# Two attention blocks on one core: which parts of x go by transfer in two jobs, and when other work is placed

## The chip, the core and the metric

The kernel runs on one core of a Trainium2 chip. The core has five engines, which run their own instruction streams and wait for each other on semaphores: TensorE (PE in the profile, with PEld for its weight loads), VectorE (DVE), ScalarE (ACT), GpSimd (POOL) and SyncE (SP, which here only issues transfers). The metric is the device time of one execution in microseconds (us), and the median of several runs is quoted.

## What is computed

The input x has 8 images of 512 channels and 32 x 32 = 1024 positions, in fp32. Two layers run one after the other, and both have the same form:

```
xn  = group_norm(x, 8 groups) * gamma + beta
q, k, v = Wq xn + bq, Wk xn + bk, Wv xn + bv      (512 x 512 weights)
a   = softmax(q^T k / 8) for each of 8 heads of 64 channels, over 1024 positions
x   = x + Wp (a v) + bp
```

All values are fp32. The result is x after the second layer.

## The kernel before

**Jobs.** A job is one image in one layer, and there are 16. Images are taken in pairs, so the order is image 0 layer 0, image 1 layer 0, image 0 layer 1, image 1 layer 1, then images 2 and 3, and so on. Jobs are numbered from 0; jobs 0 and 1 are layer 0 and jobs 2 and 3 are layer 1 of the first pair. The image stays in SBUF (the tile x) between its two layers.

**The loop.** Round n of the main loop runs the attention of job n and then the projections around it: v of job n+1 (`v_phase`), and in `deep_phases` the output projection of job n together with k and q of job n+1. Round -1 has only the projections of job 0.

**Projections by fewer products.** Each 512 x 512 projection is done in the manner of Strassen and Winograd: seven products of half size in place of eight, from sums of blocks of the input and of the weight. `FACTOR` numbers the seven weight factors. The k, q and output projections do this twice: the outer level has seven chains, taken in the order `OUTER = (1, 2, 6, 5, 7, 3, 4)`, and each chain has seven products of 128 x 256 matmuls in the order `ORDER = (1, 5, 6, 2, 7, 3, 4)`. `prepare` makes the inner factors of a weight on DVE (four sums, lines L152 to L158) at its first use, and stores them in DRAM, from where `fetch` loads them later.

**Chains, turns and queues.** A chain c fills a tile p of two halves (`put`: ACT copies two of the four quarters out of PSUM, DVE adds the other two, lines L607 and L609). In `deep_phases` two chains are always interleaved, so that a new chain begins every seven products. In its product numbers 7 and 3, which are the fifth and sixth in `ORDER`, a chain gives one turn each to other work:

```python
if ORDER[j] in (7, 3):
    if soon:
        soon.popleft()()
    elif outer:
        outer.popleft()()
    elif extra and extra[0][0] <= c:
        extra.popleft()[1]()
```

The queue `soon` holds block sums that later chains need: four steps of the inner sums (L394 to L400) and four of the output's block sums (L491 to L496). The queue `outer` holds the adds that put the outer level's results together. The queue `extra` holds loads, the output bias (`make_out_bias`, line L1023) and the norm's statistics of the job after next (line L229), each with the first chain in which it may run. What is left of `extra` runs early in the next attention.

**Outer results of the output projection.** When chain o ends, its part is added to the residual x. x has four quarters (channel half, position half). Part 1 and part 2 go to (0,0); parts 6 + 1, 5 and 3 to (0,1); parts 7 + 6 + 1 and 4 to (1,0); parts 7 + 6 + 1 and 5 to (1,1). `more(oh, sh, part, moved)` adds a part to a quarter, in one of two ways: with `moved` it issues at once a transfer on GpSimd's queue that accumulates into SBUF (line L636); without it, it queues a DVE add (line L638) in `outer`. The sums "p6 += p1" and "p7 += p6" are DVE adds in `outer` too (line L622). In layer 1 a quarter that has all its parts is sent to the output.

**Order.** PE, ACT and DVE execute in the order in which the Python code emits (`manual_schedule`), and the framework puts in the waits that the data need, in that order of emission. So an instruction that is emitted after another one on the same data waits for it, though it be a transfer. A call `later(t, fn)` emits fn once a clock, advanced by hand with each product, has moved on by t.

**Attention.** 64 steps, i = 0 to 63: PE makes the scores of step i (L817), ACT the exponential into a tile e (L822, one of six buffers), DVE adds e into acc (L832, L834), and PE multiplies by v two steps later (L848). Every eight steps end a group (L864, L871), and every two groups share a normalisation (L891 to L925). Other work comes between as chores, which `put(i, fn)` places at step i or the next free one. In round 0 these are: factors of two weights (L152 to L158), the norm of job 1 (by ACT's sums L239 and L247, then `groups`, L270 to L280, `factors`, and four `apply`, L295), the four block sums of the normed input (`sums`, L356 to L362), and the second half of the inner sums (L394 to L400).

Of the kernel before, what the change touches and what calls it, by code (L numbers as in the profile page):

```python
# [70 lines left out]
def fast_path(  # L71
# [34 lines left out]
    def later(delay, fn):  # L106
        todo.append((clock[0] + delay, fn))
# [93 lines left out]
    def used(key):  # L201
        del held[key]
        later(2.5, fetch)
# [4 lines left out]
    def x_tile(b):  # L208
        xs[b] = xpool.tile([P, NC, S], F32, tag="x", name=f"x_{b}")
        return xs[b]  # L210

    def load_x(b):
        for cc in range(NC):
            nc.sync.dma_start(xs[b][:, cc, :], x[b, cc * P : (cc + 1) * P, :])

    class Norm:
# [20 lines left out]
        def sums(self, cc):  # L237

            nc.scalar.activation(  # L239
                xn[0][:, cc, :], xs[self.b][:, cc, :], AF.Identity, accum_out=self.mv[:, cc, 0:1]  # L240
            )
# [289 lines left out]
    def deep_phases(n, extra, outs=None, early=()):  # L531
# [8 lines left out]
        def job(which):  # L540
            return n - 1 if which == O else n
# [71 lines left out]
        def end(c):  # L613
            which, o = chains[c]
            m = job(which)
            used((m, which, o))

            def p(k):
                return tiles[which, k]

            def add(to_, a, b):
                outer.append(lambda: nc.vector.tensor_add(to_, a, b))  # L622

            if which == O:
                b, layer = jobs[m]
                xt = xs[b]

                def more(oh, sh, part, moved=False):


                    cols = slice(sh * HALF, (sh + 1) * HALF)
                    to_ = xt[:, 2 * oh : 2 * oh + 2, cols]

                    def go():
                        if moved:
                            nc.gpsimd.dma_start(to_, p(part), accum_op=ALU.add)  # L636
                        else:
                            nc.vector.tensor_add(to_, to_, p(part))  # L638
                        parts[oh, sh] -= 1
                        if layer == 1 and parts[oh, sh] == 0:  # L640
                            rows = slice(oh * CH, (oh + 1) * CH)
                            later(8.0 if moved else 2.0, lambda: nc.sync.dma_start(
                                out[b, rows, cols].rearrange("(c p) s -> p c s", p=P), to_
                            ))

                    if moved:
                        go()
                    else:
                        outer.append(go)

                if o == 1:
                    more(0, 0, 1, True)
                elif o == 2:
                    more(0, 0, 2, True)
                elif o == 6:
                    add(p(6), p(6), p(1))
                    more(0, 1, 6)
                elif o == 5:
                    more(0, 1, 5)
                    more(1, 1, 5, m in (0, 2))  # L660
                elif o == 7:
                    add(p(7), p(7), p(6))
                    more(1, 0, 7)
                    more(1, 1, 7)
                elif o == 3:
                    more(0, 1, 3, True)
                elif o == 4:
                    more(1, 0, 4, True)
                return
            d = dst[which]  # L670

            def quarter(oh, sh):
                return d[:, 2 * oh : 2 * oh + 2, sh * HALF : (sh + 1) * HALF]

            if o == 2:
                add(quarter(0, 0), p(1), p(2))
            elif o == 6:
                add(p(6), p(6), p(1))
            elif o == 5:
                add(quarter(0, 1), p(6), p(5))  # L680
            elif o == 7:
                add(p(7), p(7), p(6))
                add(quarter(1, 1), p(7), p(5))
            elif o == 3:
                add(quarter(0, 1), quarter(0, 1), p(3))
            elif o == 4:
                add(quarter(1, 0), p(7), p(4))

        live, parts = {}, {(0, 0): 2, (0, 1): 3, (1, 1): 2, (1, 0): 2}
        soon, outer = deque(early), deque()  # L690
# [24 lines left out]
        at = sorted((7 * c + 2 * j, c, j) for c in range(len(chains)) for j in range(7))  # L715
        return [thunk(c, j) for _, c, j in at]

    def last_weights(n):
        w = acts.tile([P, NW, 2, CH], F32, tag="deep", name="w_last")
        nc.sync.dma_start(w, factors[O, jobs[n][1]])  # L720
        return w
# [10 lines left out]
    def last_sums(sh):  # L732


        def start():
            if sh == 0:
                tx[0] = acts.tile([P, 3, 2, HALF], F32, tag="t", name="t_last")
            nc.vector.tensor_sub(last_right(sh, 5), last_right(sh, 7), last_right(sh, 1))

        def second():  # L740
            nc.vector.tensor_sub(last_right(sh, 6), last_right(sh, 3), last_right(sh, 5))

        def third():
            nc.vector.tensor_sub(last_right(sh, 7), last_right(sh, 3), last_right(sh, 7))

        def fourth():
            nc.vector.tensor_sub(last_right(sh, 4), last_right(sh, 2), last_right(sh, 6))

        return start, second, third, fourth
# [424 lines left out]
    for n in range(-1, len(jobs)):  # L1174
        last = n + 1 == len(jobs)
        outs = None
        if n >= 0:
            chores = {}

            def put(i, fn):  # L1180
                while i in chores:
                    i += 1
                chores[i] = fn

            if last:
                w = last_weights(n)
                for i, fn in enumerate(last_sums(0)):
                    put(44 + 3 * i, fn)
            else:
                if n == 0:  # L1190
                    first_factors(put, [(O, 0), (V, 1)])
                elif n == 1:
                    first_factors(put, [(K, 1), (Q, 1)])
                elif n == 2:
                    first_factors(put, [(O, 1)])
                for i, (_, fn) in enumerate(extra):
                    put(2 + i, fn)
                at = (10, 19, 22, 24, 26, 28, 36, 39, 42, 45)
                if n == 0:
                    for i, fn in zip((3, 3, 4, 5, 6, 8, 10, 11, 12, 13, 15), reads):  # L1200
                        put(i, fn)
                    at = (22, 30, 34, 35, 37, 38, 41, 44, 47, 50)
                for i, fn in zip(at, steps + sums(n + 1)):
                    put(i, fn)
                deep_first = deep_steps(n + 1)
                for at, fn in zip((52, 54, 57, 59), deep_first[4:]):
                    put(at, fn)
                put(61, lambda: (extend_plan(n + 1), [fetch() for _ in range(RING)]))
            assert max(chores, default=0) < NT * len(att.groups)
            att.run(chores)  # L1210
            banks(0, "one")
            banks(1, "one")
            if last:
                for i, fn in enumerate(last_sums(1)):
                    later(4.1 + 1.5 * i, fn)
                later(9.9, judge)
                for sh in range(2):
                    last_proj(n, w, sh)
                break
            outs = OutputSums(n)  # L1220
            out_sums(n, outs)
            first = v_phase(n + 1, ORDER)
            for thunk in first[:-1]:
                thunk()
            rest = first[-1:]
            extra = deque()
            if jobs[n][1] == 1 and jobs[n][0] + 2 < B:
                extra.append((11, lambda b=jobs[n][0] + 2: (x_tile(b), load_x(b))))
            if n == 1:
                load, bias_steps = make_out_bias(1)  # L1230
                extra.append((8, load))
                extra.extend((11, fn) for fn in bias_steps)
            if n + 2 < len(jobs):
                reads, steps = norm_steps(n + 2)
                extra.extend((15, fn) for fn in reads)
        both = deep_phases(n + 1, extra, outs, deep_first[:4] if outs else ())
        both[0]()
        rest[0]()
        if n < 0:
            later(22.0, lambda: load_x(1))  # L1240
        for thunk in both[1:-2]:
            thunk()
        banks(0, "two")
        att = Attention(n + 1)
        att.scores(0)
        att.scores(1)
        for thunk in both[-2:]:
            thunk()
        banks(1, "two")
# [249 lines left out]
```

## Time and profile before

| | |
|---|---|
| median of 3 runs | 3214.52 us (3211.47 to 3215.15) |
| profiled execution | 3210.9 us, TensorE clock 0.999 |
| PE busy | 3191.5 us (99%), 22918 matmuls |
| DVE busy | 2774.8 us (86%), 3978 instructions |
| ACT busy | 1904.5 us (59%) |
| POOL busy | 99.4 us (3%), of which 62 transfers of 512 KB into x take 74.6 to issue |
| DMA | 313.82 MB, mean 98 GB/s |

The busy time of PE counts matmuls that overlap, so it is not a measure of how near PE is to its peak. It is still the engine that hardly stops: its waits for other engines add up to 13.6 us, and none of them lies between 692 and 3170 us. DVE is the next engine, and its busy share is an average over stages in which it is full and stages in which it is not. A row of the timeline gives start, length, engine, line, operation, output<-inputs and shapes; square brackets behind it tell how long the engine had been idle, and what released it.

### The profile page before, as it was taken

The numbers are of one execution on the slowest core, as the hardware profiler recorded it, in microseconds if no ns is written. First come the engines' busy times: TensorE is split into PE (matmuls) and PEld (weight loads), VectorE is DVE, ScalarE is ACT, GpSimd is POOL, SyncE is SP. The second block draws the span as 40 slices with busy tenths as digits, with TensorE's granted clock in tenths as the row PEclk, the third lists the DMA queues.
The fourth block names the chain that finished last, engine by engine and source line by source line (L and its number), as shares of the span: only waits on it lengthen the run. The fifth ranks groups of instructions, "written<-read, shape, count | busy, mean of one in ns | idle before, by whom it ended". The sixth has DMA issues, their size and how long they took to land.

```text
span 3210.9 us, 57782 instructions
## 1 busy us (share of the span) xinstructions
PE 3191.5 (99%) x22918; PEld 1859.8 (58%) x22918; DVE 2774.8 (86%) x3978; ACT 1904.5 (59%) x3042; POOL 99.4 (3%) x93
## 2 busy tenths in 40 slices
PE   9999999999999999999999999999999999999999
PEld 7366384563836638366483754837547375573744
DVE  8897998979889798897978889788897888978878
ACT  4746646466565665656656565565656656566564
POOL 0000000000000000000000000000000000000000
PEclk9999999999999999999999999999999999999999
DMA  9234172350613305033160421504216051150511
GB/s 316 97 104 129 68 211 70 92 170 22 210 28 88 91 27 159 22 103 128 33 208 18 115 70 34 151 16 137 100 44 194 16 138 47 49 136 19 171 37 42
DMA packets 150230, 313.82 MB, mean 98 GB/s; under 512 B 33992, under 2 KB 48960, under 8 KB 148800
## 3 DMA queue, kind: packets, MB, share of 16 engines
q1 hardware_dynamic: 133088, 277.55, 26.7%
q0 software_dynamic: 16864, 32.51, 6.2%
q8 instruction: 181, 2.97, 0.4%
q14 instruction: 97, 0.79, 0.1%
HBM read 225.13 MB, written 51.18 MB: 86 GB/s over the span
## 4 chain that ended last, share of the span: by engine, by line
PE 93%; DVE 5%; DMA 1%; issue 0%; ACT 0%; SPq 0%; POOL 0%; DVEq 0%
PE sc L817 27%; PE po L848 27%; PE vd L593 10%; PE zd L593 10%; PE z L462 6%; PE ud L593 4%; PE yd L593 4%; PE v L462 2%; PE y L462 2%; PE u L462 2%; DVE acc L834 1%; DMA x<-p 0%; PE z_last L761 0%; DVE w L154 0%; DVE p L609 0%
## 5 line engine op out<-in xcount | busy, mean ns | idle before, releaser
L822 ACT ACTIVATE e<-sc 128x1024 f32<-128x1024 f32 x1024 | 1045.7, 1023 | 582.5 <-PE sc L817 488.2
L817 PE MATMUL sc<-q,k 64*64 64x512 f32 x8192 | 1061.9, 590 | 0.0
L848 PE MATMUL po<-e,v 64*64 64x512 f32 x8192 | 1057.3, 589 | 0.0
L834 DVE TENSOR_TENSOR acc<-acc,e 128x1024 f32<-128x1024 f32 x768 | 936.1, 1219 | 57.5 <-ACT e L822 8.8
L848 PEld LDWEIGHTS po<-e,v 64*64 64x64 f32 x8192 | 313.2, 133 | 565.7 <-issue 558.4
L817 PEld LDWEIGHTS sc<-q,k 64*64 64x64 f32 x8192 | 309.9, 133 | 558.9 <-issue 545.2
L593 PE MATMUL vd<-deep,w 128*128 128x256 f32 x900 | 252.7, 380 | 1.4 <-DVE p L609 1.3
L593 PE MATMUL zd<-deep,w 128*128 128x256 f32 x892 | 248.4, 380 | 4.4 <-DVE p L607 2.4
L832 DVE TENSOR_TENSOR acc<-e,e 128x1024 f32<-128x1024 f32 x128 | 156.3, 1221 | 109.5 <-ACT e L822 109.5
L593 PEld LDWEIGHTS zd<-deep,w 128*128 128x128 f32 x892 | 168.9, 190 | 29.9 <-DVE p L607 3.7
L593 PEld LDWEIGHTS vd<-deep,w 128*128 128x128 f32 x900 | 170.6, 190 | 26.4 <-DVE p L609 2.5
L864 DVE TRANSPOSE_TENSOR_REDUCE r<-acc 128x32 f32<-128x1024 f32 x128 | 158.4, 1238 | 0.6
L636 POOL DMA_DIRECT2D x<-p x62 | 74.6, 1203 | 1971.6 <-ACT p L603 1408.4
L593 PE MATMUL vd<-os,w 128*128 128x256 f32 x420 | 118.2, 380 | 1.6 <-DVE p L609 1.5
L622 DVE TENSOR_TENSOR p<-p,p 128x1024 f32<-128x1024 f32 x94 | 114.2, 1215 | 0.0
L462 PE MATMUL z<-w,t 128*128 128x256 f32 x480 | 110.9, 379 | 0.0
L462 PE MATMUL z<-w,xn 128*128 128x256 f32 x480 | 110.1, 382 | 0.0
L413 ACT COPY ud<-vd 128x256 f32<-128x256 f32 x173 | 61.8, 357 | 77.2 <-PE vd L593 69.8
L611 ACT COPY s<-zd 128x256 f32<-128x256 f32 x173 | 64.5, 373 | 71.8 <-PE zd L593 71.7
L475 ACT COPY v<-z 128x512 f32<-128x512 f32 x32 | 18.7, 585 | 148.5 <-PE z L462 148.5
L462 PEld LDWEIGHTS z<-w,xn 128*128 128x128 f32 x480 | 90.0, 190 | 23.8 <-issue 12.2
L413 ACT COPY ud<-zd 128x256 f32<-128x256 f32 x156 | 55.7, 357 | 76.6 <-PE zd L593 75.7
(230 smaller groups left out, 4077.2 us busy)
## 6 DMA issues: line engine op xcount, KB each, us to landing
w<-deep SPq DMA_DIRECT2D x287, 448.0 KB, 3.7
w<-keep SPq DMA_DIRECT2D x129, 256.0 KB, 2.7
x<-p POOLq DMA_DIRECT2D x62, 512.0 KB, 6.9
rb<-rd SPq DMA_DIRECT2D x96, 256.0 KB, 4.0
deep<-w SPq DMA_DIRECT2D x42, 448.0 KB, 4.1
x<-x_dram SPq DMA_DIRECT2D x28, 512.0 KB, 4.3
out_dram<-x SPq DMA_DIRECT2D x28, 512.0 KB, 6.2
keep<-raw SPq DMA_DIRECT2D x5, 1792.0 KB, 7.7
```

What stands on the lines that cost most here:

```text
L413: nc.scalar.copy(u, z)
L462: nc.tensor.matmul(ps[:, ti * CH : (ti + 1) * CH], r[:, cc, t0 : t0 + P], w[:, cc, :], start=(start and ti == 0 and cc == 0), stop=(cc == ...
L593: nc.tensor.matmul(ps, lhs[:, FACTOR[i], :], moving[i], start=start, stop=True, skip_group_check=True,)
L611: return chain(product, lambda ps: nc.scalar.copy(s5, ps), put, z, y, u, w)
L622: outer.append(lambda: nc.vector.tensor_add(to_, a, b))
L636: nc.gpsimd.dma_start(to_, p(part), accum_op=ALU.add)
L817: nc.tensor.matmul(sc[h * HD : (h + 1) * HD, j, :], k[r, hp, k0 : k0 + HD], q[r, hp, sh * HALF : (sh + 1) * HALF], start=True, stop=True,)
L822: nc.scalar.activation(e, sc, AF.Exp, scale=SCALE)
L832: nc.vector.tensor_add(acc[g], self.es[i - 1], e)
L834: nc.vector.tensor_add(acc[g], acc[g], e)
L848: nc.tensor.matmul(po[g][j * HD : (j + 1) * HD, h, :], v[r, kc, d0 : d0 + HD], e[r, j, :], start=(kc == 0), stop=(kc == NT - 1),)
L864: nc.vector.tensor_reduce(self.r[:, 0, m, :], self.acc.pop(g).rearrange("p j (b e) -> p (j b) e", e=RP), AX.X, ALU.add, apply_transpose=True,)
```

## The change

The change moves work; it removes and adds no computation. It has four parts.

1. The second image is loaded 10 clock units later in round -1, so that it comes behind more of the weight factors' transfers.
2. In round 0 the norm of job 1, the block sums and the second half of the inner sums are placed at other steps of the attention, mostly sooner.
3. In the output projections of jobs 0 and 2 (`fresh`), where DVE has to prepare the output weight's factors, parts 1 and 2 of quarter (0,0) are added by DVE and no longer by transfers, and part 7 of quarter (1,1) is added by a transfer and no longer by DVE. The transfer is issued from a turn of `outer`, behind the sum "p7 += p6" which it needs.
4. The output bias of layer 1 is made in the projections behind job 0's attention, and no longer behind job 1's.

```diff
+                fresh = m in (0, 2)
                 if o == 1:
-                    more(0, 0, 1, True)
+                    more(0, 0, 1, not fresh)
                 elif o == 2:
-                    more(0, 0, 2, True)
+                    more(0, 0, 2, not fresh)
...
                     more(0, 1, 5)
-                    more(1, 1, 5, m in (0, 2))
+                    more(1, 1, 5, fresh)
                 elif o == 7:
                     add(p(7), p(7), p(6))
                     more(1, 0, 7)
-                    more(1, 1, 7)
+                    if fresh:
+                        outer.append(lambda: more(1, 1, 7, True))
+                    else:
+                        more(1, 1, 7)
...
-                    at = (22, 30, 34, 35, 37, 38, 41, 44, 47, 50)
+                    at = (20, 30, 31, 32, 34, 35, 36, 38, 40, 43)
...
-                for at, fn in zip((52, 54, 57, 59), deep_first[4:]):
+                for at, fn in zip((45, 47, 51, 53) if n == 0 else (52, 54, 57, 59), deep_first[4:]):
...
-            if n == 1:
+            if n == 0:
                 load, bias_steps = make_out_bias(1)
...
-            later(22.0, lambda: load_x(1))
+            later(32.0, lambda: load_x(1))
```

## Prediction

> **What bounds the kernel.** I read the page first: PE is busy for 3191.5 of 3210.9 us, at a clock of 0.999. Time can be won only from the few gaps of PE, and any new gap is paid in full. So the second view was the chain of waits in order of time, for the start of each attention (columns: start, length, what):
>
> ```profile
> 82.81 1.88 PE sc L817 x16
> ...
> 287.32 1.88 PE sc L817 x16
> ...
> 490.33 1.88 PE sc L817 x16
> ...
> 690.43 1.88 PE sc L817 x16
> ...
> 888.64 1.88 PE sc L817 x16
> ...
> 1086.85 1.88 PE sc L817 x16
> ```
>
> The distances are 204.5, 203.0, 200.1, then 198.2 and 198.2. The first three jobs lose 6.3, 4.8 and 1.9 us against the later ones, 13.0 in all. The attentions themselves are equal (111.3 us from 82.81 to 194.09 and from 490.33 to 601.58), so the loss lies in the projections behind them. Third view, PE's waits (us in total, times, longest):
>
> ```profile
> PE zd L593 <- DVE p L607: 3.7, 4, 1.8
> PE vd L593 <- DVE p L609: 2.8, 6, 0.6
> PE zd L593 <- DVE p L609: 2.0, 3, 1.1
> PE v L462 <- DVE q L871: 0.7, 1, 0.7
> PE zd L593 <- ACT yd L409: 0.5, 1, 0.5
> ```
>
> All are PSUM banks that DVE or ACT has not emptied in time. Fourth, the DVE timeline of job 0's output projection, and the POOL timeline of the same window:
>
> ```profile
> 239.71 0.48 DVE L609 SCALAR_TENSOR_TENSOR p<-vd,out_step,s 128x256 f32<-128x256 f32 x1
> 240.11 1.22 DVE L638 TENSOR_TENSOR x<-x,p 128x1024 f32<-128x1024 f32 x1
> 241.24 0.48 DVE L609 SCALAR_TENSOR_TENSOR p<-ud,out_step,s 128x256 f32<-128x256 f32 x1
> 241.64 1.21 DVE L622 TENSOR_TENSOR p<-p,p 128x1024 f32<-128x1024 f32 x1
> 243.23 0.48 DVE L609 SCALAR_TENSOR_TENSOR p<-zd,out_bias,s 128x256 f32<-128x256 f32 x1 [0.38 <-PE vd L593]
> 243.63 1.22 DVE L638 TENSOR_TENSOR x<-x,p 128x1024 f32<-128x1024 f32 x1
> 244.76 0.48 DVE L609 SCALAR_TENSOR_TENSOR p<-ud,out_bias,s 128x256 f32<-128x256 f32 x1
> 247.89 1.23 DVE L638 TENSOR_TENSOR x<-x,p 128x1024 f32<-128x1024 f32 x1 [2.65 <-DMA x<-p]
> ```
>
> ```profile
> 225.69 1.36 POOL L636 DMA_DIRECT2D x<-p  x1 [94.45 <-ACT yd L409]
> 234.80 1.21 POOL L636 DMA_DIRECT2D x<-p  x1 [7.75 <-DMA w<-deep]
> 236.32 1.20 POOL L636 DMA_DIRECT2D x<-p  x1 [0.31 <-ACT p L603]
> 242.26 1.20 POOL L636 DMA_DIRECT2D x<-p  x1 [4.74 <-ACT p L605]
> ```
>
> The line to read is 247.89. It is the DVE add of part 7 to quarter (1,1) of x. Part 5 was added to that quarter by the transfer issued at 236.32, which landed 11.5 us later, and DVE waited 2.65 us for it. PE then stood 1.76 us (zd at 249.50), 1.9 with the slower restart. So a DVE add that comes behind a transfer to the same quarter does wait, and all but 0.7 us of its wait reaches PE.
>
> [...] The trace has 5.1 to 11.5 us with a median of 6.9, so I use the trace; from 225 to 260 us the DMA engines were 96% busy. [...] the transfer of part 2 into quarter (0,0) went at 234.80, and that of part 1 (225.69) had landed after 8.5 us. [...]
>
> **The change part by part.**
>
> *Second input later.* The load of x for job 1 goes at 62.21 (four issues until 64.45), and the weights w<-wqkv behind it at 65.24 land only after 8.40 us. DVE waits 1.38 us for them at 73.74, and PE 1.07 at 75.21, 1.2 with the restart. Ten clock units later the load is out at about 72, behind that fetch; undisturbed the fetch takes about 6 (median of these loads), landing before DVE's 72.36. The load itself still lands near 82, before ACT reads it at 91.19. Gain: 1.2 us.
>
> *Other steps in the first attention.* The number of operations stays. DVE is without a gap from 122.37 to 236.4, so moving work inside that stretch wins nothing. One thing does: the group statistics (L270 to L274 at 128.22, 0.8 us) go three steps sooner, to about 120.8, where DVE stood idle for 1.57 us. If their gather (issued at 118.72) is there, the backlog at the end is 0.8 us shorter, and PE's wait of 0.70 at 200.23 nearly goes. If it lands late they wait no longer than the r<-r transfers behind them did, until 122.3. The sums come 3 to 7 steps sooner, onto a backlog of some 2 to 4 us; an e buffer is wanted again five steps (8.6 us) later, so PE need not stall. Gain: 0.8 us, bounds 0 and 1.5.
>
> *Layer 1's bias sooner.* Four L1023 with their accumulator reads (0.7 us each) leave job 1's projections, where DVE had no slack and PE waited 0.56 at 469.08 and 0.31 at 482.73. They go to job 0's, where DVE has a microsecond of slack in each chain after 250, which hides them. Gain: 1.0 us, bounds 0 and 1.5.
>
> *Other parts by transfer, jobs 0 and 2.* Parts 1 and 2 of quarter (0,0) become DVE adds; part 7 of (1,1) becomes a transfer: one transfer less, one DVE add more. What goes away in job 0: the 1.9 us above, and PE's wait on ACT at 244.02 (0.46, 0.6 with the restart; ACT could not write a p buffer that part 2's late transfer still read). That is 2.6 us. In job 2 neither wait was there.
>
> What it adds is order. Each chain has two turns in which DVE takes one step from the queue outer (with its 5th and 6th product), and the chains start every seven products. The first four chains' eight turns go to soon. Then in the kernel before: chain 4 takes "p6+=p1" (237.03) and the add of 6 to (0,1) (238.50); chain 5 takes the add of 5 to (0,1) (240.11) and "p7+=p6" (241.64). Only then does chain 5 end and issue part 3's transfer into (0,1), at 242.26. Chain 6 takes 7 into (1,0) (243.63) and 7 into (1,1), then issues part 4's transfer into (1,0). Every add stands before the transfer into its quarter, without a turn to spare.
>
> Now two adds enter the queue in front. Chain 4 takes 1 and 2 into (0,0); chain 5 takes "p6+=p1" and 6 into (0,1), and ends: part 3's transfer into (0,1) goes out. The add of 5 to (0,1) is still queued; chain 6 takes it three products later, and it must wait for the landing. Likewise chain 6 ends and issues part 4 into (1,0) before chain 7's turn with 7 into (1,0). Two new DVE waits of the kind at 247.89 in job 0, and two in job 2. Queued behind them on DVE are the L607 and L609 that empty PE's banks.
>
> First wait. The transfer now needs the add of 6, which ends at about 242.8, so it is issued at 243.1. Landing: part 3's transfer took 9.7, 7.3, 10.3, 10.2 and 6.2 us in jobs 0 to 4 (mean 8.7); with fewer others in flight I take 8.0, so 251.1. DVE is there at about 243.7. Wait 7.4, of which PE pays 6.7. Second wait. From the landing, DVE needs 1.13 (the add), 0.4 (L609); then part 4's p is complete and goes out 0.3 later, at +1.85. DVE does "p7+=p6" and an L607 and reaches the add of 7 at +3.0. Alone on the queue, such a transfer took 5.4 to 8.5 (part 1's: 8.5, 5.4, 7.4, 5.8, 6.1); part 7's now follows it closely, so 7.0. Wait 7.0 - 1.15 = 5.85; PE, freed at +3.0, has seven products (3.0 us) to do meanwhile, and DVE 1.9 us of work before the next bank is free: PE pays 7.0 - 2.2 = 4.8. Together 11.5 us a job, 23.0 for both. Bounds: landings of 6.2 and 5.4 give 8.1 a job, 10.3 and 8.7 give 15.5.
>
> **Sum.** 23.0 - 1.2 - 0.8 - 1.0 - 2.6 = +17.4, so 3214.5 + 17.4 = 3231.9 us.
>
> **Rivals.** (A) The new waits don't show, since the landing is early or the adds find their turn before it: then only the gains stand, -5.6, 3208.9. For it: the change lowers the transfers' number. Against: the 2.65 us at 247.89, and a shortest landing of 5.1 us against turns of 0.6 to 1.2 us behind the issue. 9%. (B) Only one wait a job costs much, the second hidden while PE and the transfers catch up: 2 x 6.7 - 5.6 = +7.8, 3222.3. 13%. (C) The first attention stalls as well, since DVE holds the e buffers, or landings are 10 us where 96% of the DMA time is taken: +28, 3242. For it job 2's 10.3 and 11.4 us; against, a stalled PE asks for no weights. 13%. The forecast itself: 65%.
>
> **Numbers.** The range of 3221 to 3243 takes in both bounds of the landings (16.2 - 7.5 to 31 - 3.0 gives 3223 to 3242) with B and C, and leaves A out. Faster by over 0.2% needs less than 3208.1: the lower part of A, 0.05. Same (to 3220.9): the rest of A and a part of B, 0.09. Slower 0.86.
>
> **What would show it.** Right: DVE L638 with two idle stretches of 5 to 8 us on DMA x<-p in each of jobs 0 and 2, each followed by a PE gap on L607 or L609; starts of attention about 213 us apart for the first pair, 202 for the second, 212 for the third; none of the 1.38 us on w<-wqkv. Wrong: no wait of L638 on x<-p, or PE running through it.

## The result, and the profile after

The changed kernel takes 3236.27 us (median of 6 runs, 3234.83 to 3237.63) against 3214.61 us before (6 runs, 3211.47 to 3215.37): a ratio of 1.0069, with a 95% interval of 1.0056 to 1.0082. It is slower by 21.7 us. 3232.0 was forecast, in a range of 3221 to 3243.

Where does the time lie? The timeline of PE in the changed kernel has the start of each attention, here of jobs 0 to 3 (start, length, what):

```profile
81.05 1.95 PE L821 MATMUL sc<-q,k 64*64 64x512 f32 x16
...
301.37 1.95 PE L821 MATMUL sc<-q,k 64*64 64x512 f32 x16
...
502.52 1.95 PE L821 MATMUL sc<-q,k 64*64 64x512 f32 x16
...
713.89 1.95 PE L821 MATMUL sc<-q,k 64*64 64x512 f32 x16
```

The same rows of the kernel before stand at 82.74, 287.25, 490.26 and 690.36. So the start is 1.7 us shorter, job 0 is longer by 15.8 (220.32 against 204.51), job 1 shorter by 1.9, and job 2 longer by 11.3. Behind that the kernels run alike: all of the loss is in jobs 0 and 2. PE's waits in the changed kernel (us in total, times, longest) name two kinds:

```profile
PE zd L593 <- DVE p L607: 18.9, 5, 9.2
PE sc L821 <- ACT e L826: 5.3, 1, 5.3
PE vd L593 <- DVE p L609: 2.2, 5, 0.6
```

The first was forecast. The second was not there before, and no step of the forecast has it. For the first, the DVE timeline of job 0's output projection:

```profile
245.77 1.21 DVE L638 TENSOR_TENSOR x<-x,p 128x1024 f32<-128x1024 f32 x1
246.90 0.47 DVE L609 SCALAR_TENSOR_TENSOR p<-zd,out_bias,s 128x256 f32<-128x256 f32 x1
257.25 1.23 DVE L638 TENSOR_TENSOR x<-x,p 128x1024 f32<-128x1024 f32 x1 [9.87 <-DMA x<-p]
258.39 0.48 DVE L609 SCALAR_TENSOR_TENSOR p<-ud,out_bias,s 128x256 f32<-128x256 f32 x1
258.78 1.22 DVE L622 TENSOR_TENSOR p<-p,p 128x1024 f32<-128x1024 f32 x1
259.92 0.42 DVE L607 TENSOR_TENSOR p<-zd,s 128x256 f32<-128x256 f32 x1
264.63 1.23 DVE L638 TENSOR_TENSOR x<-x,p 128x1024 f32<-128x1024 f32 x1 [4.30 <-DMA x<-p]
```

At 245.77 is the add of part 6 to quarter (0,1), at 257.25 that of part 5, and between them part 3's transfer into the same quarter has come: it was issued at 247.54, 0.6 us behind the end of the first add, and landed 9.7 us later. At 264.63 is the add of part 7 to (1,0), behind part 4's transfer. Job 2 has the same two waits, of 8.41 and 4.28 us. What PE made of the first one is in its timeline:

```profile
260.39 1.22 PE L593 MATMUL zd<-deep,w 128*128 128x256 f32 x2 [9.25 <-DVE p L607]
261.40 1.06 PE L593 MATMUL yd<-xn,w 128*128 128x256 f32 x2
262.25 1.06 PE L593 MATMUL vd<-t,w 128*128 128x256 f32 x2
263.11 1.06 PE L593 MATMUL vd<-deep,w 128*128 128x256 f32 x2
...
267.17 0.59 PE L593 MATMUL yd<-t,w 128*128 128x256 f32 x2
267.61 0.59 PE L593 MATMUL zd<-t,w 128*128 128x256 f32 x2
```

PE stood for 9.25 us and then worked at half its pace, 0.85 us from product to product in place of 0.43, until about 266.2. The table of windows gives the granted clock of that stretch and of the next (columns: window, length, then busy time and count of PE, PEld, DVE, ACT and POOL, then the clock, the DMA share and GB/s):

```profile
260.30:266.60 6.30, 6.12 (x14) 4.54 (x14) 2.00 (x5) 1.63 (x5) 1.54 (x2) 0.54 0.93 157
266.60:273.00 6.40, 6.36 (x29) 5.62 (x30) 3.57 (x6) 3.78 (x11) 0.00 (x0) 1.00 0.79 219
```

The second kind is in the first attention, in ACT's timeline and PE's:

```profile
136.64 1.02 ACT L826 ACTIVATE e<-sc 128x1024 f32<-128x1024 f32 x1 [0.63 <-PE sc L821]
144.00 1.24 ACT L295 ACTIVATE xn<-x,off,mul 128x1024 f32<-128x1024 f32 x1 [6.34 <-DVE off L290]
145.15 1.00 ACT L826 ACTIVATE e<-sc 128x1024 f32<-128x1024 f32 x1
```

```profile
146.21 1.98 PE L821 MATMUL sc<-q,k 64*64 64x512 f32 x8 [5.34 <-ACT e L826]
```

ACT stood 6.34 us at the first apply of the norm, which needs the factors that DVE makes in L290. The exponentials behind it in ACT's queue stood with it, and PE behind them.

### The profile page after: what moved, and what is told of

Same layout as the page of the kernel before. It is cut to its first block, busy times and chain, and to the rows that moved or that the text cites. A ratio compares the mean times of both kernels' runs of the same rounds, so it can differ in the third digit from the quotient of the medians.

```text
span 3234.5 us, 57775 instructions
## 1 busy us (share of the span) xinstructions
PE 3198.0 (99%) x22918; PEld 1863.6 (58%) x22918; DVE 2777.7 (86%) x3980; ACT 1904.8 (59%) x3042; POOL 95.6 (3%) x91
## 4 chain that ended last, share of the span: by engine, by line
PE 78%; DVE 1%; DMA 0%; issue 0%; ACT 0%; DVEq 0%
PE sc L821 22%; PE po L852 22%; PE vd L593 9%; PE zd L593 9%; PE z L462 5%; PE ud L593 4%; PE yd L593 4%; PE u L462 1%; PE y L462 1%; PE v L462 1%; PE z_last L765 0%; DMA x<-p 0%; DVE acc L838 0%; DVE q L929 0%; DVE r L868 0%; DVE x L787 0%
## 5 line engine op out<-in xcount | busy, mean ns | idle before, releaser
L638 DVE TENSOR_TENSOR x<-x,p 128x1024 f32<-128x1024 f32 x75 | 91.2, 1216 | 26.9 <-DMA x<-p 26.9
```

## The experiments

The experiments come in three groups, and each group has its own runs of the kernel before (medians 3213.98, 3214.67 and 3213.61 us). "Job 0" and so on below are distances between starts of attention as above; before they are 204.51, 203.01 and 200.10. Each distance comes from one profiled execution. Stretches that an edit doesn't touch differ by up to some 1.5 us between these executions (job 2 takes 200.86 in `p2_only` and 201.40 in `p2_late_apply`, and the nine kernels without part 1 start their first attention at 82.06 to 83.54), so a single difference of about 1 us says little.

**First group: the parts alone.**

`p3_only` has this and nothing else of the change:

```diff
+                fresh = m in (0, 2)
...
-                    more(0, 0, 1, True)
+                    more(0, 0, 1, not fresh)
...
-                    more(0, 0, 2, True)
+                    more(0, 0, 2, not fresh)
...
-                    more(1, 1, 7)
+                    if fresh:
+                        outer.append(lambda: more(1, 1, 7, True))
+                    else:
+                        more(1, 1, 7)
```

> The kernel before with part 3 alone (other parts of x by transfer in jobs 0 and 2). Theory: the inversion of order costs by itself what the two traces show for these stages, 11.3 us in job 2 and 8.4 us in the projections of job 0 (where it also takes away 2.6 us of older waits): 3214.6 + 19.7 = 3234, with two L638 waits on x<-p in each of jobs 0 and 2 and the attention of job 0 at 111.3 us. Rival (the loss comes from the parts together, for instance from DVE being later in job 0 because of its first attention): job 0 loses less than 5 us, 3228 or lower.

Measured: 3233.02 us, ratio 1.0059 (1.0042 to 1.0076). Job 0 takes 212.67 (+8.2), job 2 210.56 (+10.5). Part 3 makes this loss by itself, in both jobs. Its adds wait for transfers four times, 7.29 and 4.27 us in job 0 and 7.62 and 4.27 in job 2; PE stands 6.67 and 0.94 us in job 0, 7.00 and 1.22 in job 2.

`p2_only`:

```diff
-                    at = (22, 30, 34, 35, 37, 38, 41, 44, 47, 50)
+                    at = (20, 30, 31, 32, 34, 35, 36, 38, 40, 43)
...
-                for at, fn in zip((52, 54, 57, 59), deep_first[4:]):
+                for at, fn in zip((45, 47, 51, 53) if n == 0 else (52, 54, 57, 59), deep_first[4:]):
```

> The kernel before with part 2 alone (other steps in the first attention). Theory: the stall of 5.3 us on ACT in the first attention comes from these steps by themselves, so that attention takes 118 to 119 us in place of 111.3, and the projections behind it lose up to 1 us less: 3214.6 + 6.5 = 3221. Rival (the stall needs the later load of x or the lower load of part 3): no gap of PE on L817, 3213.5 to 3214.6.

Measured: 3220.82 us, ratio 1.0019 (1.001 to 1.0028). Job 0 takes 211.80 (+7.3), with a gap of 6.7 us on ACT in the first attention. The new steps stop PE without help from the other parts.

`p1_p4`:

```diff
-            if n == 1:
+            if n == 0:
                 load, bias_steps = make_out_bias(1)
...
-            later(22.0, lambda: load_x(1))
+            later(32.0, lambda: load_x(1))
```

> The kernel before with parts 1 and 4 alone (second input later, layer 1's bias sooner). Theory: 1.2 to 1.7 us before the first attention and 1.0 to 1.9 us in job 1's projections are won, nothing is lost in job 0: 3214.6 - 3 = 3211.5. Rival (what the traces show there came from the other parts): 3214 to 3215.

Measured: 3212.06 us, ratio 0.9995 (0.9987 to 1.0004), so no clear difference in time. In the trace the first attention starts at 81.60 (1.1 sooner), job 1 takes 201.14 (1.9 less), and job 0 gives 1.4 back (205.90), with PE waiting 2.0 us for ACT in one place. The first two don't rest on this trace alone: the five kernels with parts 1 and 4 start the first attention at 81.05 to 81.66 and take 201.12 to 201.15 for job 1, the nine without at 82.06 to 83.54 and 203.00 to 203.36. In job 0, ACT stood 2.88 us until the transfer into quarter (0,0) of the output's part 2 had landed, 9.6 us after its issue in place of 8.3 before. A load for the bias (bvb<-bv_dram, at 230.39) now goes out in front of that transfer; that it is what delays the landing isn't shown.

`no_p3` is the changed kernel with the lines of part 3 as before.

> The changed kernel with part 3 undone (parts 1, 2 and 4). Theory: jobs 0 and 2 get back 8.4 and 11.3 us, 3236.3 - 19.7 = 3216.6; the stall in the first attention stays at about 7 us. Rival (parts work together): above 3221.

Measured: 3217.65 us, ratio 1.0011 (1.0004 to 1.0018); job 2 takes 200.09 again, job 0 211.70. The parts add up within the noise: 19.0 for part 3 alone, 6.8 for part 2 and -1.9 for the rest are 23.9 us, against 21.7 measured together.

**Second group: what in part 3 and what in part 2.**

`p3_order_kept` has part 3, but each of the two transfers is emitted behind the DVE add into its quarter:

```diff
-                    more(0, 1, 5)
+                    more(0, 1, 5, then=(lambda: more(0, 1, 3, True)) if fresh else None)
...
-                    more(1, 0, 7)
+                    more(1, 0, 7, then=(lambda: more(1, 0, 4, True)) if fresh else None)
...
-                elif o == 3:
+                elif o == 3 and not fresh:
...
-                elif o == 4:
+                elif o == 4 and not fresh:
```

> Part 3 alone, but the transfers of part 3 into (0,1) and of part 4 into (1,0) are emitted directly behind the DVE adds of 5 and 7 into the same quarters. Theory: no L638 waits on x<-p, all of the 19 us of part 3 alone come back, and the 2.6 us of older waits in job 0 stay away: 3214 - 2.6 = 3211.4. Rival (part 3 costs through the load it adds on DVE, or through the transfers being late for the p buffers): 3216 or more.

Measured: 3212.96 us, ratio 0.9995 (0.9986 to 1.0003). The group of the adds into x has no idle time in front of it any more. First the changed kernel (`p3_only` has 23.5 us in 4 there), then this one:

```profile
L638 DVE TENSOR_TENSOR x<-x,p x15: 1212/1216/1226, 241.2 to 677.2; 128x1024 f32<-128x1024 f32 x15
its engine sat idle before it (us, times) until:
  DMA x<-p: 26.9, 4
```

```profile
L638 DVE TENSOR_TENSOR x<-x,p x15: 1215/1215/1220, 238.0 to 650.6; 128x1024 f32<-128x1024 f32 x15
its engine sat idle before it (us, times) until:
who waited for it (us, times):
```

With part 3's adds and transfers the same, the order of emission is worth 20 us (3233.02 in `p3_only`, 3212.96 here). So neither the added DVE work nor the other transfer is what costs. Job 0 takes 202.82, 1.7 less than before; job 2 takes 200.92, 0.8 more.

`p3_second_wait` keeps the order for part 3's transfer only, and leaves part 4's as in the change.

> Part 3 alone, with the order kept for quarter (0,1) only: part 4's transfer into (1,0) still goes in front of the DVE add of 7. Theory: one L638 wait on x<-p in each of jobs 0 and 2, of about 5 to 6 us, of which PE pays 4 to 5, since it has no slow stretch behind a first wait to hide it in: 3214 - 2.6 + 9 = 3220.5. Rival (the second wait is free, as the changed kernel's trace shows no PE gap at it): 3211.5.

Measured: 3231.89 us, ratio 1.0055 (1.0038 to 1.0072). Both theories were wrong on the size: one inverted add costs 8.0 us in job 0 and 9.8 in job 2, nearly as much as two. Its DVE, POOL and PE timelines say why:

```profile
257.61 1.22 DVE L638 TENSOR_TENSOR x<-x,p 128x1024 f32<-128x1024 f32 x1 [9.76 <-DMA x<-p]
```

```profile
246.54 3.67 POOL L636 DMA_DIRECT2D x<-p  x3 [7.20 <-ACT p L605]
```

```profile
259.62 1.22 PE L593 MATMUL vd<-deep,w 128*128 128x256 f32 x2 [7.98 <-DVE p L609]
```

The three transfers of parts 3, 4 and 7 now go out together from 246.54, and part 4's, the second, lands only some 10 us after its issue, in place of the 7.0 of the forecast. DVE waits 9.76 us, PE stands 7.98 and restarts at half pace. In the changed kernel part 4's transfer, the first of two, took 5.1 us, and part 3's, which went alone, 9.7. So the same kind of wait had no fixed price here, and that going out together makes a landing late isn't shown. What the runs show is that one stand of PE a job makes most of the loss, whichever of the two adds makes it.

`p2_late_apply` and `p2_late_groups` are part 2 with one piece put back each:

```diff
-                    at = (20, 30, 31, 32, 34, 35, 36, 38, 40, 43)
+                    at = (20, 30, 34, 35, 37, 38, 39, 40, 41, 43)
```

```diff
-                    at = (20, 30, 31, 32, 34, 35, 36, 38, 40, 43)
+                    at = (22, 30, 31, 32, 34, 35, 36, 38, 40, 43)
```

> Part 2 alone, but with the four applies of the norm on ACT at steps 35 to 38 as before, in place of 32, 35, 36 and 37 (the sums follow at 39, 40, 41 and 43; the group statistics stay at the early step). Theory: PE's 6.7 us on ACT come from ACT standing at the first apply until DVE has made the factors of the norm; three steps (5.1 us) later ACT arrives when they are nearly ready, so PE loses under 2 us in the first attention, although DVE's wait of about 4 us for rb<-rd stays: 3214 to 3216. Rival (DVE's wait for rb<-rd holds the e buffers and stops PE by itself): the stall stays at 5 us or more, 3219 to 3221.

> Part 2 alone, but with the group statistics at step 22 (23) as before; applies and sums stay at their early steps. Theory: with the statistics later, rb<-rd is issued before keep<-raw again, DVE's wait of about 4 us for it goes, and ACT's wait at the first apply shrinks from 6.8 to about 2.5 us, of which PE loses 1 to 2: 3214.5 to 3216. Rival 1 (the early apply is the whole cause): PE loses 5 us or more, 3219 to 3221. Rival 2 (the wait for rb<-rd is the whole cause): no gap on L817, 3213 to 3214.

Measured: 3218.23 us, ratio 1.0011 (1.0004 to 1.0018), and 3216.66 us, ratio 1.0006 (0.9997 to 1.0015). PE's gap on ACT falls from 6.7 to 1.9 us with the later applies and to 3.3 us with the later statistics; job 0 is still longer, by 5.8 and 5.2 us. So each piece makes a part of the stall, and both times are above the ranges that were expected. What the gap misses is in the PE timelines, of the later statistics and of the later applies:

```profile
145.56 1.99 PE L817 MATMUL sc<-q,k 64*64 64x512 f32 x8 [3.32 <-ACT e L822]
147.33 1.93 PE L848 MATMUL po<-e,v 64*64 64x512 f32 x8
149.03 1.93 PE L817 MATMUL sc<-q,k 64*64 64x512 f32 x8
150.74 1.41 PE L848 MATMUL po<-e,v 64*64 64x512 f32 x8
```

```profile
149.97 1.09 PE L817 MATMUL sc<-q,k 64*64 64x512 f32 x8 [1.90 <-ACT e L822]
150.88 1.04 PE L848 MATMUL po<-e,v 64*64 64x512 f32 x8
```

Behind the gap of 3.32 us PE runs at half pace for some 5.5 us (1.99 and 1.93 us for eight products in place of 1.04), which costs some 2.7 us more; behind 1.90 us it doesn't (1.09 and 1.04). With the later applies most of the rest comes at the end of the attention, from a DVE that is late: PE waits 2.45 us for L871, where it waited 0.70 before, and then slows down as well.

```profile
205.36 2.53 PE L462 MATMUL v<-w,t 128*128 128x256 f32 x8 [2.45 <-DVE q L871]
207.68 4.82 PE L462 MATMUL z<-w,t 128*128 128x256 f32 x16
```

From the start of the first row to the start of what follows the second, these products take 6.97 us, 1.7 more than the same ones before (5.29). DVE's lateness comes from its wait for the normalisers rb, 4.51 us in this run and 4.38 in `p2_only`, which with the later statistics isn't there. SP's queue differs between the two, first `p2_only`, then the later statistics:

```profile
125.28 0.33 SPq L908 DMA_DIRECT2D rd<-rt  x1
125.67 2.33 SPq L280 DMA_DIRECT2D mr<-dg  x2
128.10 0.54 SPq L162 DMA_DIRECT2D keep<-raw  x1
128.73 2.03 SPq L910 DMA_DIRECT2D rb<-rd  x2
```

```profile
124.46 0.33 SPq L908 DMA_DIRECT2D rd<-rt  x1
126.85 1.29 SPq L910 DMA_DIRECT2D rb<-rd  x2
128.19 0.58 SPq L162 DMA_DIRECT2D keep<-raw  x1
```

With the statistics early, the transfers that send them back (mr) and a store of 1.8 MB (keep) go in front of rb. In `p2_only` rb then landed 8.1 us after its issue, where 4.0 is the median of these transfers in the kernel before.

**Third group: the rest of part 2, and the repaired kernel.**

`p2_late_both` has statistics and applies where they were; only the sums are sooner (39, 40, 41, 43 and 45, 47, 51, 53).

> Part 2 alone with both the group statistics (step 22) and the applies (35 to 38) where they were before; only the sums (39, 40, 41, 43) and the second half of the inner sums (45, 47, 51, 53) are sooner. Theory: the earlier sums cost nothing by themselves, so no gap of PE on L817 and an attention of 111.3 us: 3213.5 to 3215. Rival (the earlier sums push DVE back and so hold up e buffers and PE): 3216 or more.

Measured: 3214.25 us, ratio 1.0003 (0.9994 to 1.0011), no gap on L817, job 0 205.40 (+0.9). The earlier sums cost nothing that the time shows.

`p2_late_store` is part 2 with the first store of factors at a later step:

```diff
-            put(at + 1, lambda i=i, which=which, layer=layer: store_factors(
+            put(at + (7 if i == 0 and len(which_layers) == 2 and (O, 0) in which_layers else 1), lambda i=i, which=which, layer=layer: store_factors(
```

> Part 2 alone, with the first of the two stores of 1.8 MB (keep<-raw) placed at step 28 in place of 22, nothing else changed. Theory: the store no longer goes in front of rb<-rd, DVE's wait of 4.4 us for it (L925) goes, ACT's wait at the first apply shrinks from 6.8 to about 3.5 us and PE's gap from 6.7 to about 2.5: first attention 114 to 117 us in place of 119, 3216 to 3219. Rival (rb<-rd is late for another reason, such as the earlier dg and mr transfers): the L925 wait and the gap stay as they are, 3221.

Measured: 3220.63 us, ratio 1.0023 (1.0014 to 1.0031), gap 6.6 us, DVE's wait for rb 4.25 us. This run doesn't decide: in SP's queue the store still went out at 126.55, in front of rb at 127.18, since SP isn't among the engines that keep the order of emission. The landing of 8.0 us in this run, too, fits a store that is still under way (7.7 us is the median of these stores in the kernel before), but whether the store or the mr transfers delay rb stays open.

`after_order_kept` is the changed kernel with the edit of `p3_order_kept`.

> The changed kernel with the order kept: part 3's and part 4's transfers are emitted directly behind the DVE adds of 5 and 7 into the same quarters. Theory: of 3236.3 about 20 us come back and only the first attention's stall of 7 us stays: 3215.5 to 3217.5. Rival (the parts together have a further cost): above 3219.

Measured: 3218.17 us, ratio 1.0014 (1.0007 to 1.002). Some 17 of the 21.7 us come back (4.6 us over this group's runs of the kernel before are left), a little less than expected: PE waits 6.8 us on ACT in the first attention, 2.5 us on ACT in job 0's projections, and in job 2 2.2 us on w<-deep. SP sent that weight right behind the four loads of the next image (from 674.66), where the kernel before sends one weight between these loads; why the order differs isn't shown.

`p14_order_kept` has parts 1 and 4 and part 3 in kept order, without part 2.

> The kernel before with parts 1 and 4 and with part 3 in kept order, without part 2. Theory: the gains add up, 1.9 us (parts 1 and 4) and 1.7 us (order kept): 3214.6 - 3.6 = 3211, faster than both kernels. Rival (gains overlap, since a PE that comes sooner waits for DVE later): 3213 or more.

Measured: 3212.41 us, ratio 0.9996 (0.9987 to 1.0004). It isn't clearly faster than the kernel before: the start (81.59) and job 1 (201.12) keep their gains, job 0 (206.18) and job 2 (201.69) lose 1.7 and 1.6, with PE waiting 2.7 us on ACT and 1.3 on w<-deep in all. The forecast that the gains add up wasn't met.

## Why the prediction was right

The waits that were forecast are there and make most of the loss, in the two jobs that were named. That the sum came so near was in part luck: terms that were too large and terms that were missing cancelled. By stretch, in us, with the measured side from one profiled execution of each kernel (their sum is 23.5; the medians differ by 21.7):

| | forecast | measured |
|---|---|---|
| before the first attention | -1.2 | -1.7 |
| job 0 | +11.5 - 2.6 - 0.8 = +8.1 | +15.8 |
| job 1 | -1.0 | -1.9 |
| job 2 | +11.5 | +11.3 |

- *Two new waits a job from the order of emission.* Right, and shown: they are there in jobs 0 and 2, they go when only the order is mended, and nothing else of part 3 costs anything that the time shows. The forecast had 11.5 us a job; part 3 alone costs 10.5 in job 2, and 8.2 in job 0, where older waits of 2.6 us go as forecast. Of the signs named, the waits were to be 5 to 8 us, each with a stand of PE behind it; they are 9.87 and 8.41 with one, and 4.30 and 4.28 without. The starts were to be 213, 202 and 212 us apart; they are 220.3, 201.2 and 211.4.
- *How a job's 11.5 us are made.* The total held by luck. The first wait was taken as 7.4 us with 6.7 on PE; `p3_only` has nearly this (7.29 and 7.62, gaps of 6.67 and 7.00), but in the changed kernel the transfer lands later than the 8.0 us taken (9.7 and 8.2), and the waits are 9.87 and 8.41, with gaps of 9.25 and 7.79. The second was taken as 5.85 with 4.8 on PE; DVE waits 4.30 and 4.28, since the transfer lands after 5.1 us in place of 7.0, and PE doesn't stop, since it is working through seven products at half pace. These cost 0.42 more each, 2.9 us, a term that the forecast doesn't have. The landings taken, 8.0 and 7.0 us, were the author's estimates from the 512 KB transfers into x of the kernel before (5.1 to 11.5 us, median 6.9); that fewer of them in flight land sooner wasn't shown.
- *The first attention.* This step failed. The forecast took a gain of 0.8 us, and said that "PE need not stall". It looked at DVE's end and at the e buffers, and not at ACT's queue: with the first apply at step 32, right behind the factors of step 31, ACT stands there until a DVE that is late gets to them. Job 0 loses 7.3 us by this part alone. It failed as well to ask what the earlier statistics would send in front of the normalisers.
- *Second input later:* 1.2 forecast, some 1.4 measured (between the means of the five and the nine starts), and DVE's wait on w<-wqkv is gone. That fetch, issued at 62.15 and now in front of the load, lands after 3.3 us in place of 8.4. *Bias sooner:* 1.0 forecast for job 1, 1.9 measured. In job 0 the forecast had it hidden by DVE's slack; there `p1_p4` gives 1.4 back, and the engine that stood was ACT, for a transfer.
- The forecast of the whole came out 4.3 us low (17.4 against 21.7): the first attention is worse than forecast by more than that, and job 1 and the start are better.
- Of the rivals, (C) had a stall in the first attention, but by e buffers; the later landings that it needed were there in part (9.7 us). So what happened is the forecast together with a part of a rival that it gave 13%.
- In the working of the range, gains of 7.5 and 3.0 us are set against the bounds of the landings; the bounds stated part by part add up to 6.8 and 3.8. That gives 3223.9 and 3241.7, inside the same range.

## What to carry to other kernels

When a transfer that accumulates into a tile and a compute add to the same tile are emitted by hand, count the turns: which is emitted first decides who waits, and three products of difference (1.3 us) cost 8 to 10 us a job here. When work of one engine is moved sooner, look at the queue of every engine that has to take its result, and at what stands behind the taker there. A gap of a busy TensorE is to be priced with its restart: 0.1 us behind the gap of 1.76 us here, and 2.9 us behind the one of 9.25.

## What was unexpected of the hardware

Behind some gaps PE goes on at half pace. Behind the gap of 1.76 us in the kernel before the granted clock was 1.00, and the first product took 0.70 us in place of 0.59. Behind 2.03 (`p1_p4`) and 2.17 us (`after_order_kept`) the rows read 0.70 and 0.59 again, with 0.43 us from product to product, and behind 1.90 us (`p2_late_apply`) 1.09 and 1.04 us for eight products, which is full pace. Behind the gap of 2.45 us in `p2_late_apply` the clock stayed at 1.00 for some 1.3 us and was then 0.50 for 3.4 us; a window inside that stretch, with the columns as above:

```profile
207.60:209.00 1.40, 1.40 (x5) 1.05 (x4) 1.37 (x4) 0.59 (x1) 0.00 (x0) 0.50 0.05 12
```

Behind gaps of 5.34, 7.79 and 9.25 us, in the changed kernel, it was 0.50 from the first product on. Behind 3.32 (`p2_late_groups`), 6.71 (`p2_only`) and 7.98 us (`p3_second_wait`) the rows take nearly twice as long: the second ones 1.93, 1.93 and 1.06 us in place of 1.04, 1.04 and 0.59. These stretches lasted 3.5 to 6.2 us. So of the gaps listed here, those up to 2.17 us were followed by full pace and those from 2.45 us on by half pace, for 3.4 us at the shortest; what ends such a stretch isn't shown. The forecast had priced these gaps as if PE went on at once.
